# 491 counted tiles instead of 363, and the first 32 gathers taken from x itself

## The chip, the cores and the metric

The program runs on one NeuronCore of a Trainium2 chip. TensorE multiplies matrices, VectorE and ScalarE do elementwise work, GpSimd (POOL) issues the gathers, and SyncE and ScalarE issue the plain DMAs; all run side by side and wait for each other by semaphores. The metric is the device time of one execution in microseconds, the median of several runs.

## The reference

Two graph layers on 12,500 nodes with 32 features and 200,000 edges, sorted by destination. Cut to what matters here:

```
h = relu(layernorm(x))
# layer 0: a normalised sum over neighbours
h0  = h * rsqrt(max(out_degree, 1))
agg = segment_sum(h0[src], dst)
x   = x + agg * rsqrt(max(in_degree, 1)) @ W + b
# layer 1: an MLP over every edge
h   = relu(layernorm(x))
msg = concat(h[dst], h[src] - h[dst])
m   = relu(relu(relu(msg @ W1 + b1) @ W2 + b2) @ W3 + b3) @ W4 + b4
x   = x + segment_sum(m, dst) / max(count(dst), 1)
```

`edge_attr_4` isn't used.

## The kernel before

Edges are cut into 1563 tiles of 128 (`NTR`) and 391 chunks of four tiles (`NCH`, `TPC`). The edges are sorted by destination, so the destinations of chunk g lie in a window of 128 nodes that begins near 32 g (`STEP`, `W`); a flag checks this, and a general path behind `tc.If` stands for other data. The order of the instructions on each engine is the one written out (`manual_schedule`); each engine works in order.

**The start** (lines 137 to 445). x is loaded in four pieces, normalised on VectorE with square roots on ScalarE, and written to the table `tab_h` in DRAM, 33 columns with a one in the last. Then the out-degree of every node is counted: for each tile VectorE makes two one-hot matrices of the source number (its high and low part, lines 331 and 332) and TensorE multiplies them into `deg_ps`. Beside this GpSimd gathers the rows of the first 64 chunks (`EARLY`) from `tab_h` into `rows_early`, whose degree factor isn't known yet. When the degrees are there, a second table `tab_hn` is written: the rows times their factor, each as the sum of three bf16 terms, and a one.

**Layer 0's loop** (lines 754 to 772) runs over m from 64 to 302 and takes the edges in three ways at once:

- *Gathered chunks.* Chunks 64 to 299 (`DIR` is 300) are gathered from `tab_hn`, four gathers of 128 rows for each turn of the loop, into one of eight buffers `rows`. Two turns later `sum_rows` multiplies each tile by its one-hot of the destination and adds four chunks into one PSUM bank `ps_late`; `add_rows` then adds the bank to the sums in SBUF (`Sums.add`, line 528: columns that are new are copied by ScalarE, the others added by VectorE).
- *Early chunks.* Every third turn (`LATER`) a `scale_rows` is begun for one of the first 64 chunks. It has steps of one turn each: a load of the source's high parts (`srow`), a one-hot of them, 12 look-up matmuls into the PSUM bank `look`, then four masked reductions that give each edge its factor, the product, and its split into three bf16 terms by turns of ScalarE and VectorE; then the row sums into a bank `ps_early`, and after every fourth chunk the addition.
- *Counted tiles.* The remaining 363 tiles (`ND`, from chunk 300 on) aren't gathered. `count_edges` makes for each tile a matrix of how often each source node meets each of the tile's 13 destinations: one-hots on VectorE (`oh`, `lo`), and for each of three parts ("thirds") a count matmul of 128 x 429 or 128 x 416 into `count_ps` and its eviction to SBUF on ScalarE (lines 738 to 743). `multiply` then multiplies the counts of eight tiles by the whole table, 98 matmuls, five or six behind each third of the next tiles, and puts the result in place with two small matmuls in `st2`.

`stages` and `steps` spread the thirds evenly over the loop's turns. Node updates (`update_nodes`) follow as sums become complete, one step a turn; they write the tables `tab_i` and `tab_j` of layer 1. [...]the loop uses `ps_late`, `ps_early`, `look`, `st2`, two of `count_ps`, one of the node updates, and `kept`.

**Layer 1's loop** gathers all 1563 tiles from `tab_j` and runs the MLP, two chunks a turn. It begins when the last node update has been written.

Of the kernel before, what the change touches and what calls it, by code (L numbers as in the profile page):

```python
# [8 lines left out]
F32 = mybir.dt.float32  # L9
BF16 = mybir.dt.bfloat16  # L10
# [6 lines left out]
P = 128  # L17
# [41 lines left out]
QE = EARLY // (GRP * J)  # L59

DIR = 300
ND = NTR - DIR * TPC
# [18 lines left out]
def gnn_kernel(  # L83
# [73 lines left out]
    for at in pieces:  # L157
        nc.sync.dma_start(xp[:, at, :], parts(xa)[:, at, :])
    nc.scalar.dma_start(src_i, src_t)
    nc.scalar.dma_start(dst_i, dst_t)  # L160
# [44 lines left out]
    nc.gpsimd.memset(w1s[D:, HID:], 0.0)  # L205

# [36 lines left out]
    src_j = stay.tile([P, NT], I32, name="src_j")  # L245

    def gather(tile_ap, table, col):
        nc.gpsimd.indirect_dma_start(  # L248
            out=tile_ap, out_offset=None, in_=table,
            in_offset=bass.IndirectOffsetOnAxis(ap=col, axis=0))  # L250

# [27 lines left out]
    with tc.tile_pool(name="deg", bufs=3) as hp, tc.tile_pool(  # L279
# [31 lines left out]
        deg_ps = pp.tile([P, PART], F32, name="deg_ps")  # L311
        gathered, batches = 0, list(range(0, NTR, HG * HT))

# [9 lines left out]
        for b in batches:  # L323
            to = min(EARLY, -(-EARLY * (b // (HG * HT) + AHEAD_HG) // len(batches)))
            if to > gathered:
                c = slice(gathered * TPC, to * TPC)
                nc.vector.tensor_scalar(src_j[:, c], src_i[:, c], OFF, None, op0=OP.add)
                for g in range(gathered, to):
                    gather_chunk(rows_early[:, g], tab_h[:, :], g)
                gathered = to  # L330
            hi = one_hots("hi", 0, PART, b)
            lo = one_hots("lo", 1, P, b)
            for t in range(b, min(NTR, b + HG * HT)):
                g, i = divmod(t - b, HT)
                nc.tensor.matmul(deg_ps, lo[:, g, :, i], hi[:, g, :, i], start=(t == 0), stop=(t == NTR - 1))
        nc.vector.tensor_scalar(src_j[:, EARLY * TPC :], src_i[:, EARLY * TPC :], OFF, None, op0=OP.add)
        deg = hp.tile([P, PART], F32, name="deg", bufs=1)
# [243 lines left out]
    with tc.tile_pool(name="e0", bufs=8) as sp, tc.tile_pool(name="nu", bufs=1) as np_, tc.tile_pool(  # L581
# [28 lines left out]

        def hot_ahead(g, name="hot", bufs=AHEAD + 4):
            hots[g] = one_hots(sp, rel_h[:, g * TPC : (g + 1) * TPC], W, name, bufs)

        def sum_rows(g):
            k, i = divmod(g, GRP)
            if i == 0:
                group_ps[k] = pp.tile([D3, SPAN], F32, name="ps_late" if g >= EARLY else "ps_early")
            ps, rows, hot = group_ps[k], rows_of.pop(g), hots.pop(g)
            for t in range(TPC):
                nc.tensor.matmul(  # L620
                    ps[:, STEP * i : STEP * i + W], rows[:, t, :], hot[:, t // 2, :, t % 2], start=(i == 0 and t == 0),
                    stop=(i == GRP - 1 and t == TPC - 1), skip_group_check=True)
# [8 lines left out]
        def scale_rows(g):  # L631
# [5 lines left out]
            turned = sp.tile([PART, CHUNK], BF16, name="sturned", bufs=2)  # L637
            nc.vector.tensor_scalar(turned, row, part_s[:PART], None, op0=OP.is_equal)
            yield
            ps = pp.tile([P, TPC, P], F32, name="look")  # L640
            for t in range(TPC):
# [5 lines left out]
            for t in range(TPC):  # L647
# [5 lines left out]
            scaled = ps[:, 0, :].rearrange("p (t c) -> p t c", t=TPC)  # L653
            nc.vector.tensor_tensor(
                scaled, rows_early[:, g, :, :D], w[:, :, None].to_broadcast([P, TPC, D]), op=OP.mult)
            rows = rows_of[g] = sp.tile([P, TPC, D3], BF16, name="rows_scaled", bufs=2)
            nc.scalar.activation(rows[:, :, 3 * D :], rows_early[:, g, :, D:], AF.Copy)
            for k in range(3):
                part = rows[:, :, k * D : (k + 1) * D]
                nc.scalar.activation(part, scaled, AF.Copy)  # L660
                if k < 2:
                    nc.vector.tensor_sub(scaled, scaled, part)
            hot_ahead(g, "hot_e", 2)
            yield
            sum_rows(g)
            yield
            add_rows(g)

# [53 lines left out]
        def count_edges():  # L722
# [4 lines left out]
            for i in range(ND):  # L727
                g, t = divmod(i, TD)
                if t == 0:
                    for _ in before:  # L730
                        yield
                    if g > 0:
                        before = multiply(g - 1)
                    counts[g] = dp.tile([P, TD, PART, WD], BF16, name="count", bufs=2)
                if i % 2 == 0 and i + 2 < ND:
                    onehots_of(i + 2)
                oh, lo = onehots[i // 2], los[i // TPC]
                for k, (a, b) in enumerate(THIRDS):
                    n = (b - a) * WD
                    ps = pp.tile([P, KW], F32, name="count_ps", bufs=2)  # L740
                    nc.tensor.matmul(ps[:, :n], lo[:, i % TPC // 2, :, i % 2], oh[:, k, :n, i % 2], start=True, stop=True)  # L741
                    nc.scalar.activation(  # L742
                        counts[g][:, t, a:b, :], ps[:, :n].rearrange("p (h d) -> p h d", d=WD), AF.Copy)
                    next(before, None)
                    yield
# [337 lines left out]
```

## Time and profile before

| what | value |
|---|---|
| median of 3 runs | 4330.28 us (4326.65 to 4355.74) |
| the profiled execution | 3552.55 us |
| its span, first to last instruction | 3550.7 us |
| mean granted TensorE clock | 0.812 |
| first gather from `tab_h` (256 in all) | 48.56 us |
| first gather of `rows` (944) | 375.85 us |
| first gather of `gj` (1563) | 1572.77 us |
| last gather of `gj` starts at | 3522.8 us |
| count matmuls (1089), first and last start | 329.6 and 1467.0 us |

A line of the page's groups gives the source line, the engine, the operation with what it writes and reads, how often, the busy time and the mean of one, and the idle time of that engine just before with what ended most of it. A busy share says nothing of what an engine waits for; the views of waits and of single instructions do. POOL's gathers are DMAs[...].

### The profile page before, as it was taken

To read this page: it belongs to the slowest core of one execution; us is meant where nothing else is said; L and a number is where in the kernel's file an instruction comes from. 1 tells how busy PE (TensorE), PEld (TensorE's weight loads), DVE (VectorE), ACT (ScalarE), POOL (GpSimd) and SP (SyncE) were. 2 spreads that over 40 slices of the span, in tenths; PEclk is the share of its full clock that TensorE was granted. 3 is DMA by queue.
4 is the path that set the end of the run, shared out by engine and by line. 5 is a ranking of instruction groups with operands and counts; after the bars stand their busy time and mean duration, and the time that the engine had idled before them with its cause. 6 is when DMAs were issued, how large, how long until landed. Compare 5 with 4: busy or idle time off the path is not lost. (4 is left out here: it accounts for less than half of the span.)

```text
span 3550.7 us, 50481 instructions
## 1 busy us (share of the span) xinstructions
PE 2630.5 (74%) x18596; PEld 1780.9 (50%) x18596; DVE 1669.8 (47%) x4150; ACT 1103.2 (31%) x2552; POOL 2616.8 (74%) x2782
## 2 busy tenths in 40 slices
PE   3871567777777777637888788877788877887787
PEld 2650355555555555514555555544455545554455
DVE  8995456667666665313333333333333333333333
ACT  0002355656656655301212222222212222222212
POOL 3777777777777777767777777777777777777775
PEclk9999998888888888657767877778867788778878
DMA  4113111111211111212222222222222222222221
GB/s 88 15 15 76 24 28 31 32 35 33 38 30 34 33 34 27 45 34 59 61 61 62 61 61 61 61 59 60 61 61 62 61 61 61 61 58 61 61 61 32
DMA packets 238327, 173.61 MB, mean 49 GB/s; under 512 B 157666, under 2 KB 186562, under 8 KB 238074
## 3 DMA queue, kind: packets, MB, share of 16 engines
q0 software_dynamic: 88416, 79.16, 12.4%
q1 hardware_dynamic: 131306, 85.26, 8.8%
q10 hardware_dynamic: 18352, 5.89, 0.9%
q8 instruction: 150, 2.46, 0.3%
q14 instruction: 103, 0.84, 0.1%
HBM read 157.18 MB, written 12.92 MB: 48 GB/s over the span
## 5 line engine op out<-in xcount | busy, mean ns | idle before, releaser
L248 POOL DMA_INDIRECT gj<-tab_j,src_j x1563 | 1474.9, 944 | 493.8 <-issue 414.8
L248 POOL DMA_INDIRECT rows<-tab_hn,src_j x944 | 891.8, 945 | 287.7 <-issue 200.5
L742 ACT ACTIVATE count<-count_ps 128x429 bf16<-128x429 f32 x1089 | 545.0, 525 | 368.7 <-PE count_ps L741 347.1
L845 PE MATMUL p<-ident,gj 128*128 128x128 f32 x784 | 243.6, 351 | 400.6 <-DMA gj<-tab_j,src_j 398.8
L878 DVE TENSOR_TENSOR h<-p,b3n 128x512 f32<-128x512 f32 x196 | 135.3, 690 | 811.5 <-PE p L875 811.5
L875 PE MATMUL p<-w3s,h 128*128 128x64 f32 x3128 | 483.0, 319 | 0.0
L875 PEld LDWEIGHTS p<-w3s,h 128*128 128x128 f32 x3128 | 453.9, 231 | 50.2 <-issue 41.2
L866 ACT ACTIVATE h<-p,b2s 128x512 f32<-128x512 f32 x391 | 247.3, 683 | 739.5 <-PE p L863 739.5
L741 PE MATMUL count_ps<-oh,lo 128*128 128x429 bf16 x1089 | 433.1, 409 | 47.2 <-ACT count L742 33.1
L845 PEld LDWEIGHTS p<-ident,gj 128*128 128x128 f32 x784 | 118.0, 161 | 662.4 <-issue 641.4
L696 PEld LDWEIGHTS <-table 128*128 128x128 bf16 x4508 | 352.3, 109 | 132.2 <-issue 74.8
L696 PE MATMUL st<-count,table 128*128 128x104 bf16 (+1 forms) x4508 | 414.9, 233 | 0.1
L620 PE MATMUL ps_late<-hot,rows 128*97 128x128 bf16 x944 | 166.3, 255 | 306.7 <-DMA rows<-tab_hn,src_j 243.7
L893 PEld LDWEIGHTS ps<-hot,h 128*64 128x64 f32 x3126 | 277.5, 193 | 170.1 <-issue 157.0
L248 POOL DMA_INDIRECT rows_early<-tab_h,src_j x256 | 246.7, 964 | 124.4 <-issue 53.3
L853 ACT ACTIVATE h<-p 128x512 f32<-128x512 f32 x196 | 117.0, 597 | 689.4 <-PE p L849 689.4
L849 PE MATMUL p<-turned,ai 128*64 128x512 f32 x782 | 322.3, 915 | 0.0
L893 PE MATMUL ps<-hot,h 128*64 128x128 f32 x3126 | 306.4, 361 | 0.5 <-DVE h L878 0.5
L685 DVE TENSOR_TENSOR oh<-keys,kept 128x858 bf16<-128x858 f16 x546 | 291.7, 590 | 7.0 <-PE count_ps L741 6.9
L620 PEld LDWEIGHTS <-rows 128*97 128x97 bf16 x944 | 103.5, 138 | 361.5 <-DMA rows<-tab_hn,src_j 293.3
L863 PE MATMUL p<-h,w2s 64*128 64x512 f32 x782 | 263.9, 755 | 0.0
L829 DVE TENSOR_TENSOR turned<-row,kept 128x512 f32<-128x512 f16 x391 | 249.8, 680 | 25.1 <-PE p L849 20.3
(186 smaller groups left out, 2426.2 us busy)
## 6 DMA issues: line engine op xcount, KB each, us to landing
row<-rel_row SPq DMA_DIRECT2D x195, 256.0 KB
gj<-tab_j,src_j POOLq DMA_INDIRECT x1563
rows<-tab_hn,src_j POOLq DMA_INDIRECT x944
ai<-tab_i SPq DMA_DIRECT2D x195, 64.0 KB
srow<-hi_row SPq DMA_DIRECT2D x64, 98.0 KB
rows_early<-tab_h,src_j POOLq DMA_INDIRECT x256
tab_j<-nu_aij SPq DMA_DIRECT2D x24, 128.0 KB
tab_i<-nu_aij SPq DMA_DIRECT2D x24, 128.0 KB
```

The source lines that it names most:

```text
L248: nc.gpsimd.indirect_dma_start(out=tile_ap, out_offset=None, in_=table, in_offset=bass.IndirectOffsetOnAxis(ap=col, axis=0))
L620: nc.tensor.matmul(ps[:, STEP * i : STEP * i + W], rows[:, t, :], hot[:, t // 2, :, t % 2], start=(i == 0 and t == 0), stop=(i == GRP - 1 ...
L685: nc.vector.tensor_tensor(oh[:, k, :n], keys[:, k, None, i : i + 2].to_broadcast([P, n, 2]), count_h[:, :n], op=OP.is_equal)
L696: nc.tensor.matmul(ps[:, : tiles * WD], table[:, h, :], c[:, :tiles, h, :], start=(h == 0), stop=(h == PART - 1))
L741: nc.tensor.matmul(ps[:, :n], lo[:, i % TPC // 2, :, i % 2], oh[:, k, :n, i % 2], start=True, stop=True)
L742: nc.scalar.activation(counts[g][:, t, a:b, :], ps[:, :n].rearrange("p (h d) -> p h d", d=WD), AF.Copy)
L829: nc.vector.tensor_tensor(turned, v["row"][:, k], part_f.to_broadcast([P, CHUNK]), op=OP.is_equal)
L845: nc.tensor.matmul(p1[:, t, :], v["gj"][:, t].rearrange("p k c -> p (k c)"), ident, is_transpose=True, start=(t == 0), stop=False, skip_gr ...
L849: nc.tensor.matmul(p1[k * HID : (k + 1) * HID].rearrange("p t e -> p (t e)"), v["ai"][:, k], v["turned"][k], start=False, stop=True, skip_ ...
L863: nc.tensor.matmul(p2s[k], w2s[s, :], v["h1"][s, :], start=True, stop=True)
L875: nc.tensor.matmul(p3[:, k * TPC + t, :], v["h2"][k][:, t * P : (t + 1) * P], w3s, start=True, stop=True)
L893: nc.tensor.matmul(ps[k * HID : (k + 1) * HID, o : o + W], v["h3"][:, k * TPC + t, :], v["hot"][k][:, t, :], start=(i == 0 and t == 0), st ...
```

## The change

- `DIR` goes from 300 to 268: chunks 64 to 267 are gathered (816 gathers instead of 944), and 491 tiles instead of 363 are counted. The loop over m has 32 turns fewer, and `stages` and `steps` follow.
- `count_ps` has three banks instead of two.
- The bank comes from `ps_early`, which is gone: each early chunk's row sums go into columns of its own `look` bank and are added chunk by chunk.
- The first 8 chunks (`RAW`) are gathered from x itself (`xa`), straight after the memsets on GpSimd and before the layer norm, with the unshifted indices `src_i`; the load of `src_i` is cut so that their 32 columns come first. The ones in the last column are written by a memset. `scale_rows` normalises these rows edge by edge: mean and variance of each gathered row, and the factor times 1 / sd. The product takes the positive part in the same instruction, for all early chunks.
- The spread of the other early gathers over the degree count begins at chunk 8.

```diff
+RAW = 8
-DIR = 300
+DIR = 268
...
-    nc.scalar.dma_start(src_i, src_t)
+    for c in (slice(0, RAW * TPC), slice(RAW * TPC, NT)):
+        nc.scalar.dma_start(src_i[:, c], src_t[:, c])
...
+    nc.gpsimd.memset(rows_early[:, :RAW, :, D:], 1.0)
+    for c in range(RAW * TPC):
+        gather(rows_early[:, c // TPC, c % TPC, :D], xa, src_i[:, c : c + 1])
...
-        gathered, batches = 0, list(range(0, NTR, HG * HT))
+        gathered, batches = RAW, list(range(0, NTR, HG * HT))
...
-            to = min(EARLY, -(-EARLY * (b // (HG * HT) + AHEAD_HG) // len(batches)))
+            to = min(EARLY, RAW + -(-(EARLY - RAW) * (b // (HG * HT) + AHEAD_HG) // len(batches)))
...
-        nc.vector.tensor_scalar(src_j[:, EARLY * TPC :], src_i[:, EARLY * TPC :], OFF, None, op0=OP.add)
+        for c in (slice(0, RAW * TPC), slice(EARLY * TPC, NT)):
+            nc.vector.tensor_scalar(src_j[:, c], src_i[:, c], OFF, None, op0=OP.add)
...
-                group_ps[k] = pp.tile([D3, SPAN], F32, name="ps_late" if g >= EARLY else "ps_early")
+                group_ps[k] = pp.tile([D3, SPAN], F32, name="ps_late")
...
+            h = rows_early[:, g, :, :D]
+            if g < RAW:
+                m = sp.tile([P, TPC], F32, name="raw_m", bufs=2)
+                nc.vector.tensor_reduce(m, h, AX.X, OP.add)
+                nc.vector.tensor_scalar(m, m, 1.0 / D, None, op0=OP.mult)
+                nc.vector.tensor_sub(h, h, m[:, :, None].to_broadcast([P, TPC, D]))
+                square = sp.tile([P, TPC, D], F32, name="raw_sq", bufs=2)
+                nc.scalar.activation(square, h, AF.Square)
             yield
+            if g < RAW:
+                nc.vector.tensor_reduce(m, square, AX.X, OP.add)
+                nc.vector.tensor_scalar(m, m, 1.0 / D, EPS, op0=OP.mult, op1=OP.add)
+                sd = sp.tile([P, TPC], F32, name="raw_sd", bufs=2)
+                nc.scalar.activation(sd, m, AF.Sqrt)
...
-            nc.vector.tensor_tensor(
-                scaled, rows_early[:, g, :, :D], w[:, :, None].to_broadcast([P, TPC, D]), op=OP.mult)
-            rows = rows_of[g] = sp.tile([P, TPC, D3], BF16, name="rows_scaled", bufs=2)
+            if g < RAW:
+                nc.vector.reciprocal(m, sd)
+                nc.vector.tensor_tensor(w, w, m, op=OP.mult)
+
+            nc.vector.scalar_tensor_tensor(
+                scaled, h, 0.0, w[:, :, None].to_broadcast([P, TPC, D]), op0=OP.max, op1=OP.mult)
+            rows = sp.tile([P, TPC, D3], BF16, name="rows_scaled", bufs=2)
...
-            hot_ahead(g, "hot_e", 2)
+            hot = one_hots(sp, rel_h[:, g * TPC : (g + 1) * TPC], W, "hot_e", 2)
             yield
-            sum_rows(g)
+            total = ps[:D3, 1]
+            for t in range(TPC):
+                nc.tensor.matmul(
+                    total, rows[:, t, :], hot[:, t // 2, :, t % 2], start=(t == 0), stop=(t == TPC - 1))
             yield
-            add_rows(g)
+            sums.add(slice(0, D3), STEP * g, total)
+            added([g])
...
-                    ps = pp.tile([P, KW], F32, name="count_ps", bufs=2)
+                    ps = pp.tile([P, KW], F32, name="count_ps", bufs=3)
```

## The prediction

> **What bounds the kernel now.** I read the page's busy rows and slices first, then the costliest groups, then the waits inside the stage that the change touches, then single instructions there.
>
> ```profile
> PE 2630.5 (74%) x18596; PEld 1780.9 (50%) x18596; DVE 1669.8 (47%) x4150; ACT 1103.2 (31%) x2552; POOL 2616.8 (74%) x2782
> ...
> POOL 3777777777777777767777777777777777777775
> ...
> L248 POOL DMA_INDIRECT gj<-tab_j,src_j x1563 | 1474.9, 944 | 493.8 <-issue 414.8
> L248 POOL DMA_INDIRECT rows<-tab_hn,src_j x944 | 891.8, 945 | 287.7 <-issue 200.5
> ```
>
> POOL shows the same digit from the first gather to the end. A 7 is not slack: each gather is 944 ns of work and 0.30 us of "issue", so one starts every 1.248 us, and a slice of such gathers is a 7. The view of POOL in order of time shows that, and a hole at the start:
>
> ```profile
> 48.56 1.10 POOL L248 DMA_INDIRECT rows_early<-tab_h,src_j  x1 [44.20 <-DMA b3n<-in_b]
> 49.96 0.95 POOL L248 DMA_INDIRECT rows_early<-tab_h,src_j  x1 [0.30 <-issue]
> 51.21 0.94 POOL L248 DMA_INDIRECT rows_early<-tab_h,src_j  x1 [0.30 <-issue]
> ```
>
> 2763 gathers of 1.248 us are 3448 of the span's 3550.7 us; the rest is mostly this hole, 18 us between the two layers and 28 us behind the last gather. So the gathers set the time, and only in layer 0's loop (375.9 us, the first gather of `rows`, to 1572.8, the first of `gj`) does the change take any away. What the other engines have left there is told by the waits between 400 and 1460 us (engine, line, what was waited for: us in total, times, longest):
>
> ```profile
> ACT count L742 <- PE count_ps L741: 297.0, 349, 4.0
> PEld L620 <- DMA rows<-tab_hn,src_j: 190.2, 207, 3.1
> ...
> PE ps_late L620 <- DMA rows<-tab_hn,src_j: 155.1, 177, 2.9
> ...
> DVE look L662 <- ACT rows_scaled L660: 112.7, 126, 4.4
> ...
> PE ps_late L620 <- ACT acc_t L542: 55.9, 31, 5.1
> ...
> PE count_ps L741 <- ACT count L742: 26.3, 46, 3.9
> ```
>
> TensorE waits for gathered rows for 155 to 190 of these 1060 us (its two rows see partly the same gap). That is all the slack there is: take gathers away and give counts, and it is used up. The same stretch by engine (busy us and count of PE, PEld, DVE, ACT, POOL; clock; DMA):
>
> ```profile
> 400.00:1460.00 1060.00, 795.60 (x7717) 591.73 (x7714) 660.57 (x2099) 634.23 (x1618) 801.58 (x849) 0.85 0.18 32
> ```
>
> **Two rules of the Trainium skill.** "TensorE: Matmul & The Clock Gate", section on HAM oscillation, says that a gap of more than about 3.4 us puts TensorE back to half clock, and that it then needs about as long to recover. The trace agrees:
>
> ```profile
> 902.63 0.58 PE L620 MATMUL ps_late<-hot,rows 128*97 128x128 bf16 x4 [3.72 <-ACT acc_t L542]
> ...
> 908.57 2.46 ACT L742 ACTIVATE count<-count_ps 128x416 bf16<-128x416 f32 x5 [0.17 <-PE count_ps L741]
> ```
>
> After the 3.72 us gap a third of a counted tile (one count matmul and five or six table matmuls) takes 0.79 us; from 908.6 on it takes 0.49, which is also ScalarE's pace (five evictions in 2.46 us). I go by these two numbers. "SBUF — State Buffer", section "Who interferes with whom", says that VectorE operations in a two-port mode, or with two SBUF inputs, block GpSimd. The 32 new gathers lie beside the layer norm, which is full of such operations. The trace of before doesn't show a cost: between 100 and 200 us VectorE is busy for 100.00 us and POOL starts 81 gathers, the same as elsewhere. I go by the trace.
>
> **The change, part by part.** Sums are made against the profiled execution: 3552.55 us, the span and 1.85 us around it. The median of the runs, 4330.28, is 778 us longer, and no view shows where. I carry the difference in microseconds over unchanged, and price the other reading as a rival.
>
> (1) 32 raw gathers. They need `xa` and 32 columns of `src_i`, whose load is now first on ACT's queue, and are issued behind the memsets that end at 4.4 us. 32 x 1.248 = 39.9 us fit into the hole of 44.2, so the other 224 early gathers start at 48.6 as before and end 39.9 us sooner. Next comes `tab_hn`: its last write is issued at 290.5 us, so the row gathers can start at 336 instead of 375.9. Gain at POOL 39.9 us (bounds: 0, if the gathers were blocked, to 44.2). One more memset (nearest, `hx` 0.32 us) and one more DMA issue on ACT's queue (nearest, SP's of `srow`, 0.31 to 0.34 us) lie in the hole; the added `src_j` operation (0.2 us) is before any gather that reads it.
>
> (2) 128 gathers fewer: 128 x 1.248 = 159.7 us of POOL. With (1), gathers alone would put the first `gj` at 1572.8 - 199.6 = 1373.
>
> (3) 128 counted tiles more: 384 thirds (384 count matmuls, 384 evictions, 1568 table matmuls), 16 more groups with their two transposes, and 192 VectorE one-hots of 0.59 us and 32 of 0.41. On VectorE 126 us, on ScalarE 384 x 0.49 = 188, on TensorE the same 188. Against it stand 128 row-sum matmuls fewer, in 32 iterations fewer of the loop.
>
> (4) TensorE's chain. 1060 less 155 to 190 us of gather waits is 870 to 905 us for 1048 thirds and 212 loop iterations. The thirds at 0.49 us are 514; the remaining 356 to 391 us (row sums, look-ups, node updates, stalls, cold clock) are 1.68 to 1.84 per iteration. After: 1473 x 0.49 = 722, and 204 x 1.68 to 1.84 = 343 to 375, in all 1065 to 1097, middle 1081. Counting begins at 329.6 us, and nothing ahead of it changes but some 1 us for longer keys; so it ends near 1411. The loop's last sums, the last group and the last node updates follow; of before only the last part shows unpaced (last row gather at 1554.0 to `gj` at 1572.8, 18.8 us), so I take 35 (bounds 19 and 60). First `gj` at 1446: 127 us sooner. Chain (1411 + 35) and gathers (1373) don't add; the later one counts.
>
> (5) The third count bank. It can win at most the 26.3 us that TensorE waits for an eviction, and some of the clock; below nothing it can't go, since it only removes waits.
>
> (6) Early sums by chunk. 64 additions instead of 16: VectorE + 48 x 0.25 = 12 us, ScalarE + 64 x 0.19 - 16 x 0.27 = 8 us, both with idle time (VectorE 400 of 1060 us, ScalarE 426). But the sum now lies in `look`'s only buffer, so the next chunk's 12 look-up matmuls wait for the addition issued just ahead of them. Behind them stand four row sums and all counts. The nearest row is the wait for `acc_t` (55.9 / 31 = 1.8 us, longest 5.1). ScalarE's copy stands behind at most three evictions, 1.5 us. Bounds 0 to 64 x 5.1 = 326 us; I take 64 x 0.4 = 26, which (5) pays.
>
> (7) Normalising eight chunks: on VectorE 8 x (0.29 + 0.17 + 0.31 + 0.29 + 0.18 + 0.17 + 0.16), the node update's rows of the same shapes, 12.6 us; on ScalarE 8 x (0.31 + 0.21) = 4.2. Hidden by the same idle time; if it is gone, 17 us.
>
> Sum: -127 us, 3425 for a profiled execution, **4203** for the median. ScalarE then has 92 us (634.2 less 542.5 of evictions) + 722 + 12 = 826 us of work in 1081, VectorE 331 (660.6 less 329.5 of one-hots for 349 tiles) + 329.5 x 491 / 349 + 25 = 820. All three are near their limit, and waits that were harmless can show.
>
> **Rivals.** *The gathers still set the pace.* If the unexplained 778 us lie in the gathers (0.28 each, 1.53 us in an unprofiled run), 816 row gathers take 1248 us, the chain's 1081 hide behind them, and the change gives 128 x 1.53 + 44 = 240: 4090. For it: nothing else is repeated evenly enough. Against: the profile shows 1.248 everywhere.
>
> *The coupling eats the gain.* ScalarE and VectorE wait for each other in each scaled chunk (112.7 and 46.0 us of waits), three engines work in order at 75 to 80%, and the chain comes to some 1180 us: 4300, no change that can be told.
>
> *Slower, by the look-up bank.* At (6), each scaled chunk costs what the wait for `acc_t` cost at its worst in the quoted lines, 3.7 us, enough to drop the clock: 64 x 3.7 = 237 instead of 26, 4330 - 127 + 211 = 4414. It decides from 2.4 us a chunk (26 + 127 = 153 over 64); over 1% slower from 3.1. For it: ScalarE is in order, and copies stand behind evictions. Against: with three banks that queue is short.
>
> *Slower, by the clock.* If the 778 us are a TensorE at half clock in unprofiled runs, it is the bound, and 384 x 0.79 less 128 x 0.15 gives +284: 4614. The profile's 0.85 speaks against it.
>
> **How the numbers follow.** Likeliest, the chain at 4155 to 4270: 0.43. Gathers pace, 4080 to 4130: 0.27. Coupling, within 43 us (1%, about what measuring this kernel can tell from no change): 0.15. Slower: look-up bank 0.10, clock 0.05. So faster 0.70, same 0.15, slower 0.15. The range 4080 to 4320 leaves out the slower cases and the ends of the others.
>
> **What would show it.** First gather near 5 us; first row gather near 336; first `gj` near 1446, then unchanged to the end; in the loop fewer than 81 gathers per 100 us, POOL waiting for TensorE's row sums rather than only for "issue"; TensorE's wait for rows almost gone; clock above 0.85. Wrong would be: 81 gathers per 100 us all the way and `gj` near 1373; look-up matmuls waiting over 2 us for the `acc_e` copy; a gap between median and profile that changes by more than 50 us.

## The result: 51 us slower, and two kinds of chip

The changed kernel takes **4379.9 us** (median of 9, 4369.8 to 4386.8) beside 4328.9 for the kernel before (median of 9, 4316.3 to 4355.7). The ratio is **1.0109** [1.0087, 1.0130]: slower by 1%, where 3% faster had been forecast.

One thing has to be known to read any number below: the kernel before takes about 4330 us on some chips and about 3551 us on others, steadily, and the profiled execution of the prediction (3552.55 us) was of the second kind while the times it forecast from (4330.28) were of the first. Of the five chips that ran the experiments, one was of the 3551 kind and four of the 4330 kind. Each was used in one session, so the runs can't tell a lasting property of a chip from a state that it was in; "kind of chip" stands for either. Every kernel is compared with the kernel before on the same chip; "beside 4330" and "beside 3551" say which kind that was.

### The profile page after: what moved, and what is told of

The parts are those of the page before. It is cut to its first block, busy times and chain, and to the rows that moved or that the text cites. A ratio compares the mean times of both kernels' runs of the same rounds, so it can differ in the third digit from the quotient of the medians.

```text
span 4370.6 us, 54919 instructions
## 1 busy us (share of the span) xinstructions
PE 2953.7 (68%) x20468; PEld 1939.2 (44%) x20468; DVE 1792.5 (41%) x4473; ACT 1279.9 (29%) x3034; POOL 2501.2 (57%) x2655
## 4 chain that ended last, share of the span: by engine, by line
PE 35%; another core or an unknown queue 11%; issue 10%; DVE 4%; POOL 3%; ACT 2%; DMA 1%; ACTq 0%; DVEq 0%; POOLq 0%
PE p L905 9%; PE p L893 6%; PE p L879 5%; PE ps L923 5%; PE p L875 3%; POOL gj L211 3%; PE count_ps L771 2%; PE st L726 2%; ACT count L772 1%; DVE hot L575 1%; DVE turned L859 1%; DVE h L908 1%; PE kept L836 1%; PE ps_late L628 0%
## 5 line engine op out<-in xcount | busy, mean ns | idle before, releaser
L211 POOL DMA_INDIRECT rows<-tab_hn,src_j x816 | 771.8, 946 | 793.2 <-PE ps_late L628 281.5
L772 ACT ACTIVATE count<-count_ps 128x429 bf16<-128x429 f32 x1473 | 716.9, 527 | 508.4 <-PE count_ps L771 289.1
L771 PE MATMUL count_ps<-oh,lo 128*128 128x429 bf16 x1473 | 585.5, 421 | 180.7 <-ACT count L772 69.1
L726 PEld LDWEIGHTS <-table 128*128 128x128 bf16 x6076 | 480.2, 110 | 328.7 <-issue 254.4
L726 PE MATMUL st<-count,table 128*128 128x104 bf16 (+1 forms) x6076 | 565.4, 234 | 14.3 <-ACT acc_d L550 6.3
L893 PE MATMUL p<-h,w2s 64*128 64x512 f32 x782 | 384.4, 840 | 70.6 <-issue 69.0
L715 DVE TENSOR_TENSOR oh<-keys,kept 128x858 bf16<-128x858 f16 x738 | 393.7, 589 | 80.5 <-PE count_ps L771 39.0
L342 PE MATMUL deg_ps<-hi,lo 128*128 128x98 bf16 x1563 | 175.8, 271 | 195.1 <-DVE lo L325 147.3
L575 DVE TENSOR_TENSOR hot<-rel_h,kept 128x512 f32<-128x512 f16 x391 | 249.2, 678 | 0.0
L342 PEld LDWEIGHTS <-lo 128*128 128x128 bf16 x1563 | 131.0, 126 | 240.0 <-DVE lo L325 177.1
```

The lines of the kernel that those rows point to most:

```text
L211: nc.gpsimd.indirect_dma_start(out=tile_ap, out_offset=None, in_=table, in_offset=bass.IndirectOffsetOnAxis(ap=col, axis=0))
L715: nc.vector.tensor_tensor(oh[:, k, :n], keys[:, k, None, i : i + 2].to_broadcast([P, n, 2]), count_h[:, :n], op=OP.is_equal)
L726: nc.tensor.matmul(ps[:, : tiles * WD], table[:, h, :], c[:, :tiles, h, :], start=(h == 0), stop=(h == PART - 1))
L772: nc.scalar.activation(counts[g][:, t, a:b, :], ps[:, :n].rearrange("p (h d) -> p h d", d=WD), AF.Copy)
L893: nc.tensor.matmul(p2s[k], w2s[s, :], v["h1"][s, :], start=True, stop=True)
```

## The profile after

The page of the changed kernel, taken beside 4330: busy rows, POOL's slices, and the two groups of gathers.

```profile
PE 2953.7 (68%) x20468; PEld 1939.2 (44%) x20468; DVE 1792.5 (41%) x4473; ACT 1279.9 (29%) x3034; POOL 2501.2 (57%) x2655
...
POOL 6554355444554444554666666666666666666663
...
L211 POOL DMA_INDIRECT gj<-tab_j,src_j x1563 | 1477.9, 946 | 882.3 <-issue 437.8
L211 POOL DMA_INDIRECT rows<-tab_hn,src_j x816 | 771.8, 946 | 793.2 <-PE ps_late L628 281.5
```

POOL is no longer a row of 7s. A gather still takes 0.946 us, but half of POOL's time in layer 0 is waiting, and most of that is not "issue". In layer 1, where nothing was changed, it waits too. The waits from 400 to 2030 us (engine, line, what was waited for: us in total, times, longest):

```profile
POOL rows L211 <- PE ps_late L628: 281.5, 70, 6.5
...
DVE look L687 <- ACT rows_scaled L685: 193.3, 105, 7.0
POOL rows L211 <- issue: 191.5, 624, 0.6
POOL rows L211 <- PE count_ps L771: 184.9, 76, 6.6
...
PE look L664 <- ACT acc_e L550: 89.0, 45, 3.8
...
POOL rows L211 <- PE c_ps L451: 62.0, 1, 62.0
```

The gathers wait for TensorE, 281.5 us for the row sums that free their buffers and 184.9 for counts. TensorE's wait for gathered rows, 155 us in the profile of the prediction, is not among the longer waits. One wait of 62 us for `c_ps`, a small product behind the degree stage, holds the first row gather until 480.8 us. The look-up matmuls wait 89 us for the addition of the early sums: that line is new, and it is the one that the prediction had named as a sign of being wrong (over 2 us each was its mark; 89.0 / 45 is 2.0).

How different the two kinds of chip are shows best in the degree stage, in code that the change leaves alone. Below are the stretches 60 to 260 and 500 to 1900 us of the changed kernel (busy us and count of PE, PEld, DVE, ACT, POOL; clock; DMA share; GB/s), and after them 60 to 260 us of two kernels whose degree stage is that of the kernel before: `half_gj`, an experiment below, beside 4330, and the kernel before itself, profiled again on the chip of the 3551 kind.

```profile
60.00:260.00 200.00, 93.72 (x835) 69.72 (x832) 117.19 (x238) 0.00 (x0) 115.53 (x123) 1.00 0.13 14
500.00:1900.00 1400.00, 987.20 (x9451) 727.00 (x9450) 766.37 (x2365) 799.04 (x2064) 708.75 (x750) 0.81 0.14 22
```

```profile
60.00:260.00 200.00, 84.82 (x755) 63.31 (x756) 106.44 (x221) 0.00 (x0) 121.72 (x129) 1.00 0.11 12
```

```profile
60.00:260.00 200.00, 164.03 (x1463) 122.40 (x1462) 200.00 (x426) 0.00 (x0) 150.91 (x160) 1.00 0.13 15
```

835 and 755 matmuls against 1463 in the same 200 us, all at a granted clock of 1.00; VectorE is busy 117 and 106 us rather than 200. No instruction takes longer on VectorE, ScalarE or POOL (a gather 946 ns and 944, the 128x512 eviction on ScalarE 685 and 684); the time lies between the instructions.

## Experiments

Times are medians in us; the ratio is to the kernel before on the same chip. "First `gj`" is where layer 1's gathers begin.

| kernel | beside | time | ratio | first row gather | first `gj` |
|---|---|---|---|---|---|
| before_now | 3551 | 3554.9 | one run | 374.6 | 1571.4 |
| raw_only | 3551 | 3516.7 | 0.9906 [0.9889, 0.9922] | 338.7 | 1536.4 |
| counted_only | 3551 | 3525.7 | 0.9930 [0.9913, 0.9947] | 377.9 | 1546.2 |
| banks_only | 3551 | 3551.3 | 1.0003 [0.9994, 1.0012] | 375.3 | 1572.2 |
| changed_now | 4330 | 4391.7 | 1.0144 [1.0111, 1.0177] | 481.5 | 2035.1 |
| changed_b | 4330 | 4386.5 | 1.0131 [1.0091, 1.0170] | 482.2 | 2037.3 |
| changed_c | 4330 | 4377.5 | 1.0114 [1.0090, 1.0139] | 480.6 | 2029.8 |
| raw_only_b | 4330 | 4302.9 | 0.9944 [0.9930, 0.9958] | 479.9 | 1949.9 |
| raw_counted | 4330 | 4348.1 | 1.0051 [1.0032, 1.0069] | 477.0 | 1993.9 |
| two_banks | 4330 | 4402.1 | 1.0174 [1.0152, 1.0196] | 479.3 | 2049.1 |
| banks_only_b | 4330 | 4332.8 | 1.0002 [0.9985, 1.0020] | 506.1 | 1977.1 |
| after_284 | 4330 | 4317.9 | 0.9977 [0.9961, 0.9992] | 481.6 | 1966.3 |
| after_332 | 4330 | 4438.0 | 1.0265 [1.0240, 1.0289] | 474.6 | 2083.6 |
| half_table | 4330 | 4220.7 | 0.9732 [0.9696, 0.9769] | 483.3 | 1875.2 |
| half_rows | 4330 | 4089.0 | 0.9443 [0.9422, 0.9464] | 479.2 | 1732.0 |
| third_bf16 | 4330 | 4276.0 | 0.9879 [0.9837, 0.9922] | 504.7 | 1984.4 |
| half_gj | 4330 | 3362.6 | 0.7779 [0.7750, 0.7808] | 502.1 | 1971.5 |
| raw_third | 4330 | 4249.2 | 0.9818 [0.9787, 0.9850] | 479.8 | 1953.6 |

**The kernel before again: where are the 778 us?** No edit.

> The kernel before, unedited, profiled once more. Theory A (the profiled execution of 3552 us was not like the timed ones, and every stage of a timed one is longer by stalls of the consuming engines): a span near 4330 us, the first row gather at some 420 to 480 us rather than 375.9, the first gj at some 1950 to 2000 us, and POOL waiting over 200 us for the row sums in layer 0's loop, as in the profile of the changed kernel. Rival B (the two kernels really differ as the two profiles show, and 778 us lie outside the profiled span): a span near 3550 us again, the first gj near 1573, POOL waiting for 'issue' only.

Its span was 3553.1 us on a chip where its timed runs take 3551. The span is the one that rival B expected, but the timed runs there take 3551 us too, so no 778 us lie outside it, and both A and B fall for this chip. The changed kernel's profiled span, 4370.6 us, likewise agrees with its own timed runs. The gap was not between profiled and timed executions; it was between chips.

third_bf16 and half_gj, below, are the kernel before up to the end of layer 0, so their traces tell where it stands beside 4330: first row gather at 503 us rather than 375 (+128), first `gj` at 1971 to 1984 rather than 1571 (another +273 to +283). Layer 1's gathers then span 2314 to 2332 us in every trace beside 4330 that leaves it alone, 2320 in the middle, rather than 1950 (+370). Together that is the gap.

**The parts, beside 3551.**

```diff
-DIR = 300
+DIR = 268
```

> Only DIR = 268, so 128 tiles are counted that were gathered; early sums in groups, two count banks, no raw gathers. Theory A (in a timed execution TensorE, ScalarE and VectorE set the pace of layer 0, and a counted tile costs them more than its gather saved): slower than before, by 50 to 120 us (128 x 0.4 to 0.9). Rival C (the slowdown is that of the early sums in the look-up bank): this part alone is faster by 50 us or more. The recorded forecast by its own steps: some 100 us faster.

25 us faster, so neither theory A, nor rival C, nor the forecast's 100 us. The waits from 400 to 1460 us show what the removed gathers left:

```profile
POOL rows L248 <- issue: 171.8, 562, 0.6
...
POOL rows L248 <- PE count_ps L741: 113.6, 104, 5.9
PE count_ps L741 <- ACT count L742: 106.9, 100, 4.7
...
POOL rows L248 <- PE ps_late L620: 30.2, 17, 4.3
```

The gathers now wait for TensorE, and TensorE for ScalarE's evictions: 107 us rather than the 26.3 of before. Counting lasts from 333.6 to 1471.8 us and the first `gj` comes 74 us after that.

The raw gathers alone (the new gathers, their normalising, the split index load; DIR 300, two banks, early sums in groups):

> Only the 32 raw gathers with their normalising; DIR stays 300, early sums in groups, two count banks. Theory A: the end of the early gathers is not what the row gathers wait for (that is VectorE and TensorE in the degree stage), so within 20 us of the kernel before. The recorded forecast by its own steps: POOL ends 39.9 us sooner, so 20 to 44 us faster.

34 us faster; theory A falls. Layer 0's row gathers of this kernel (count, min/median/max ns, first and last start):

```profile
L211 POOL DMA_INDIRECT rows<-tab_hn,src_j x944: 940/944/1063, 338.7 to 1516.6; - x189
```

They start at 338.7 us rather than 374.6. Here the forecast's step held.

The third bank and the early sums by chunk, at DIR 300:

```diff
-                    ps = pp.tile([P, KW], F32, name="count_ps", bufs=2)
+                    ps = pp.tile([P, KW], F32, name="count_ps", bufs=3)
...
-            sum_rows(g)
+            total = ps[:D3, 1]
+            for t in range(TPC):
+                nc.tensor.matmul(
+                    total, rows[:, t, :], hot[:, t // 2, :, t % 2], start=(t == 0), stop=(t == TPC - 1))
             yield
-            add_rows(g)
+            sums.add(slice(0, D3), STEP * g, total)
+            added([g])
```

> Only the third count bank and the early sums by chunk in the look-up bank; DIR stays 300, no raw gathers. Theory A: the two are near even, -30 to +30 us. Rival C (each scaled chunk stalls TensorE for the addition): slower by 64 x 2 to 64 x 4 = 128 to 256 us, with look-up matmuls waiting over 2 us for the acc_e copy. The recorded forecast: 0, since 26 us are won and 26 lost.

No difference. The look-up matmuls' wait for the addition is there (27.3 us, 57 times, longest 1.0), beside 178.5 us of TensorE's waits for gathered rows, behind which it is probably hidden. The third bank's own gain is in the same zero, so the recorded forecast's reading, as much won as lost, is not excluded.

**The whole, and the parts again, beside 4330.**

> The changed kernel, unedited, beside a kernel before of the same session. In the session of the first experiments the kernel before takes 3551 us, as its profiled execution did, not 4329. Theory A2 (two conditions of the chip: at 3551 the gathers are near the bound and the change gains; at 4329 every stage of TensorE, VectorE and ScalarE is drawn out, gathers wait for them, and the change loses 51 us): if the kernel before takes 3551, the changed one takes 3491 or less (raw gathers -34, counted tiles -25, added), and 3425 if the recorded forecast's sum held. If the kernel before takes 4329, the changed one takes 4380. Rival D (the changed kernel itself falls into the drawn-out form, whatever the session): 4370 beside 3551.

> The changed kernel, unedited, once more, for a session of the other kind: so far the kernel before took 3551 us in the first session and 4331 in the second, on another chip, while the parts were measured in the first and the whole in the second. Theory F (a chip on which TensorE is held back takes 4331; there the end of layer 0 is TensorE's, on the other the gathers'): where the kernel before takes 3551, the changed one takes 3491 or less (the sum of the parts, -59), and where it takes 4331, 4380 to 4392 again. Rival D (the changed kernel itself falls into the drawn-out form): 4370 or more in both.

> The changed kernel, unedited. It has been timed on chips where the kernel before takes 4330, never where it takes 3551. Theory F: 3491 or less beside 3551; 4380 to 4392 beside 4330.

All three came to stand beside 4330 and repeat the result: +49 to +60 us. So rival D is not excluded by them: the whole change was never timed beside 3551, where its parts add up to -58 (-34, -25, +1).

The raw gathers alone:

> Only the 32 raw gathers, DIR 300, two count banks, early sums in groups; for a session of the other kind. Theory F: beside 3551 it was 3517 (-34). Beside 4331 the row gathers wait for the degree stage's TensorE (62 us in the changed kernel's trace), so -10 to +10. The recorded forecast by its own steps: -20 to -44 in both.

26 us faster, within the forecast's -20 to -44, and theory F's -10 to +10 fell. The first row gather comes 22 to 26 us sooner (479.9 against 502.1 to 506.1 in the kernels with the early gathers of before) although it waits 61 us for `c_ps`.

The third bank and the early sums by chunk at DIR 300:

> Only the third count bank and the early sums by chunk, DIR 300; for a session of the other kind. Beside 3551 it was 3551 (0). Theory G (on the chip where TensorE is held back, the early sums in the look-up bank lengthen a chain that nothing hides): 20 to 60 us slower than before, since with 491 tiles the changed kernel was 44 slower than the same kernel with groups and two banks. Rival (the 44 us are only of the many counted tiles): -15 to +15.

Nothing in sum, as the rival said. So what costs in the whole must need the 491 tiles. The changed kernel with early sums in groups and two banks, and with early sums by chunk and two banks:

> The changed kernel with two count banks and early sums in groups: the raw gathers and the 128 further counted tiles alone. Theory A2: the bank is worth more with 491 tiles than with 363, since counts waited 102 us for evictions in the kernel with counted tiles only (26 us before): 10 to 60 us slower than the changed kernel. Rival C (early sums by chunk cost TensorE stalls, hidden while gathers set the pace, visible with 491 tiles): 20 to 100 us faster than the changed kernel.

> The changed kernel with two count banks rather than three; early sums by chunk in the look-up bank stay. Beside 4330 the same kernel with groups and two banks took 4348, the changed one 4386 to 4392, so 40 us lie in one of the two. Theory G (the early sums in the look-up bank): 4380 to 4400, no better than the changed kernel. Rival J (the third bank lets counts run ahead of the row sums that free the gathers' buffers): 4340 to 4355. Beside 3551: theory F says 5 to 40 us slower than the changed kernel.

Going from kernel to kernel by the ratios (1% is 43 us; the whole at the mean of its three, 1.0130):

- 32 raw gathers: 0.9944, -24 us
- 128 counted tiles more: 0.9944 to 1.0051, **+46 us**
- early sums by chunk, at 491 tiles and two banks: 1.0051 to 1.0174, **+53 us**
- the third bank: 1.0174 to 1.0130, -19 us

Sum +56, by construction the mean of the three repeats (the first result was +51). The kernels stood on different chips of the kind; the changed kernel's own three ratios scatter by 13 us. Two differences can be taken on one chip: two_banks is 25 us above changed_c, and changed_now 44 above raw_counted (+53 - 19 by the ratios). Theory G holds where tiles are many: two_banks came out above the changed kernel, not at 4340 to 4355, so the bank helps and the early sums cost. Two lines of the waits of two_banks, 400 to 2040 us:

```profile
PE count_ps L771 <- ACT count L772: 110.6, 137, 4.5
...
PE look L664 <- ACT acc_e L550: 57.8, 45, 3.1
```

With groups the second line doesn't exist. The first is 117.8 us there, so the early sums do not show in the counts' own wait; they put the look-up's wait ahead of everything behind it on TensorE.

**Which way do counted tiles pay?** The changed kernel with 64 or 256 tiles moved back to gathers:

```diff
-DIR = 268
+DIR = 284
```

> The changed kernel with DIR = 284: 64 tiles fewer are counted and 64 more gathered, 80 us of POOL at 1.248 us each. Theory A2, session of 3551: the engines, not the gathers, end layer 0 at DIR = 268, so within 20 us of the changed kernel, faster by up to 20; session of 4329: faster than the changed kernel by some 20 to 30 us (half of what 128 tiles cost). Rival E (gathers still set the pace at DIR = 268): slower than the changed kernel by up to 80 us.

```diff
-DIR = 268
+DIR = 332
```

> The changed kernel with DIR = 332: 256 tiles fewer are counted (235 in all) and 256 more gathered, 320 us of POOL. Theory A2, session of 3551: gathers alone set layer 0, from 336 us on 1072 row gathers of 1.248 us, so the first gj near 1680 and some 3660 us in all, 170 slower than the changed kernel. Session of 4329: POOL is waiting there anyway, so faster than the changed kernel by 30 to 100 us. Rival E: slower by 320 us in both.

At 284 it is 74 us faster than the changed kernel on the same chip, over twice what was expected, and 10 us faster than before. At 332 it is slower than both, where 30 to 100 us less had been expected: fewer counts and more gathers there do not mean less time. In the stretch 500 to 1900 us of after_332 (same columns as before) TensorE is busy a quarter less than in the changed kernel, and its granted clock is 0.63 rather than 0.81:

```profile
500.00:1900.00 1400.00, 749.31 (x5771) 572.14 (x5771) 574.30 (x1986) 441.71 (x1249) 889.06 (x941) 0.63 0.16 26
```

So a tile's price is not one number. Of the three values tried with the changed kernel 284 is the best; 300 was run only with parts of the change. Why 332 is so bad was not taken apart.

**TensorE or gathers?** The changed kernel without every second table matmul, so that its counted sums are incomplete:

```diff
-                    nc.tensor.matmul(
-                        ps[:, : tiles * WD], table[:, h, :], c[:, :tiles, h, :], start=(h == 0), stop=(h == PART - 1))
+                    if h % 2 == 0:
+                        nc.tensor.matmul(
+                            ps[:, : tiles * WD], table[:, h, :], c[:, :tiles, h, :], start=(h == 0), stop=(h == PART - 2))
```

> The changed kernel without every second table matmul (L726: 49 of the 98 of each counted group, so 3038 of 6076, some 263 us of TensorE's busy time at 0.087 us each; the counted sums are then incomplete). All gathers, evictions and one-hots stay. Theory F, beside 4330 (layer 0 ends with TensorE): first gj 150 to 300 us sooner, 4090 to 4240. Rival K (ScalarE, VectorE or semaphores end it): within 50 us of the changed kernel. Beside 3551: 50 to 150 us sooner than the changed kernel, down to where the gathers of layer 0 end (first gj 1373).

The changed kernel with half of layer 0's row gathers; the rows of two tiles stand in for four, so its sums are other numbers:

```diff
-                gather_chunk(rows_of[m], tab_hn[:, :], m)
+                for t in range(TPC // 2):
+                    c = m * TPC + t
+                    gather(rows_of[m][:, t, :], tab_hn[:, :], src_j[:, c : c + 1])
...
-                    ps[:, STEP * i : STEP * i + W], rows[:, t, :], hot[:, t // 2, :, t % 2], start=(i == 0 and t == 0),
+                    ps[:, STEP * i : STEP * i + W], rows[:, t % 2, :], hot[:, t // 2, :, t % 2], start=(i == 0 and t == 0),
```

> The changed kernel with two gathers for each chunk of layer 0's loop rather than four; the row sums read each gathered tile twice, so TensorE, ScalarE and VectorE have the same work and POOL 408 x 1.248 = 509 us less. Theory F, beside 4330: the gathers are hidden behind TensorE, so within 40 us of the changed kernel (4340 to 4400). Rival (the gathers still set the pace of layer 0): 4000 to 4250. Beside 3551: between; if TensorE ends layer 0 there too, within 30 us.

half_table gives 157 us for 3038 matmuls, as theory F said. half_rows gives **289 us** for 408 gathers, and theory F fell. The time is in the rival's range, yet that gathers set the pace does not fit the trace: in the changed kernel no wait of TensorE for gathered rows is among the longer ones, and in half_rows POOL waits longer for TensorE than it did with all gathers (526 us for counts alone between 500 and 1600 us, 143 before). The stretch 500 to 1600 us, first of changed_c, then of half_rows:

```profile
500.00:1600.00 1100.00, 768.71 (x7363) 567.29 (x7363) 597.01 (x1841) 619.54 (x1605) 555.06 (x589) 0.82 0.14 22
```

```profile
500.00:1600.00 1100.00, 852.67 (x9234) 639.61 (x9234) 745.41 (x2312) 759.67 (x2021) 340.78 (x360) 0.91 0.11 19
```

With 229 gathers fewer in the stretch, TensorE gets through 9234 matmuls rather than 7363. The gathers slow TensorE without its waiting for their data. This does not hang on the releasers, of which the traces beside 4330 miss many (half_gj has 20,392 semaphore updates on record, before_now 63,134): all the idle time in front of the row sums is 87.8 us in the changed kernel, and 297.2 in before_now, where the gathers do set the pace.

**The same in layer 1, where nothing else of the change lies.** The kernel before with half of layer 1's gathers (each gathered tile is used twice):

```diff
-                gather_chunk(gj[:, :, k, :], tab_j[:, :], g)
+                for t in range(min(TPC // 2, NTR - g * TPC)):
+                    c = g * TPC + t
+                    gather(gj[:, t, k, :], tab_j[:, :], src_j[:, c : c + 1])
...
-                    p1[:, t, :], v["gj"][:, t].rearrange("p k c -> p (k c)"), ident, is_transpose=True,
+                    p1[:, t, :], v["gj"][:, t % 2].rearrange("p k c -> p (k c)"), ident, is_transpose=True,
```

> The kernel before with two gathers for each chunk of layer 1 rather than four (782 rather than 1563); TensorE's transposes read each gathered tile twice, so all other work is the same. Theory L (beside 4330 the gathers' traffic itself holds TensorE back: in the degree stage TensorE starts 7.3 matmuls per us where little is gathered and 2.9 where much is, beside 3551 it is 7.2 and 7.3): layer 1, 2317 us there and TensorE's by its waits, comes near the 8 to 9.5 us of TensorE work in each of 196 steps, 1570 to 1860 us, so 3570 to 3900 in all. Rival M (TensorE is held back there by itself, whatever is gathered): it waits for gathers for only some 30 us of layer 1, so within 60 us of the kernel before. Beside 3551 both say 3170 to 3450, since there layer 1 has the gathers' pace.

970 us faster. Theory L holds, and the gain is beyond its range: rival M's 60 us is far off. Layers 0 of the two kernels agree (first `gj` at 1971.5 and, with all gathers, 1977 to 1984), so this is not a better chip. In layer 1, first changed_c (2100 to 4300 us), then half_gj (2100 to 3300):

```profile
2100.00:4300.00 2200.00, 1630.60 (x8272) 967.73 (x8272) 639.62 (x1263) 396.27 (x777) 1404.91 (x1490) 0.70 0.23 51
```

```profile
2100.00:3300.00 1200.00, 1097.26 (x7830) 724.28 (x7832) 600.84 (x1202) 358.28 (x742) 656.29 (x697) 0.91 0.30 69
```

6.5 matmuls per us rather than 3.8. A step of layer 1 (196 of them) takes 6.9 us of the span of the gathers rather than 11.8. The clock rises too, from 0.70 to 0.91; whether that is a cause or follows from fewer standstills isn't separated. Here again TensorE was not waiting for the data: its idle time before the matmuls that read gathered rows, first in before_now, then in the changed kernel, is the smaller on the slow kind.

```profile
L845 PE MATMUL p<-ident,gj 128*128 128x128 f32 x784 | 244.3, 350 | 407.0 <-DMA gj<-tab_j,src_j 405.1
```

```profile
L875 PE MATMUL p<-ident,gj 128*128 128x128 f32 x784 | 210.1, 365 | 177.7 <-issue 136.8 <-DMA gj<-tab_j,src_j 39.5
```

The degree stage has no such test, but the same association, with a delay. Counted by half microseconds from 60 to 400 us of half_gj, TensorE starts 2.1 matmuls per us where six or more gathers began in the 8 us before, and 6.2 where at most four did. In before_now six or more stand before nearly every stretch, and it starts 7.3.

**Less work for TensorE in layer 1.** The kernel before with the third product in bf16:

```diff
+    nc.scalar.activation(w3b, w3s, AF.Copy)
...
-                h2 = ep.tile([P, CHUNK], F32, name=f"h2{k}")
+                h2 = ep.tile([P, CHUNK], BF16, name=f"h2{k}")
...
-                        p3[:, k * TPC + t, :], v["h2"][k][:, t * P : (t + 1) * P], w3s, start=True, stop=True)
+                        p3[:, k * TPC + t, :], v["h2"][k][:, t * P : (t + 1) * P], w3b, start=True, stop=True)
```

> The kernel before with the messages' third product in bf16 (h2 written as bf16, a bf16 copy of w3): the 16 matmuls of a step in layer 1 take some 0.5 us rather than 2.0, gathers and all else stay, and the rounding differs. Theory F: where the kernel before takes 3551, layer 1 has the pace of its gathers (1563 x 1.248 = 1950 us), and nothing changes, -10 to +10; where it takes 4331, layer 1 is TensorE's, and 196 steps with 1.5 us less give -100 to -300. Rival H (there the gathers or the semaphores of layer 1 are slow, not TensorE's work): within 30 us in both.

53 us, less than theory F's 100 and more than rival H's 30: 0.27 us a step of the 1.5 that the expectation counted. What may take its place shows in order of time. From layer 1 of this kernel, all engines (start us, us, engine, line, operation, and in brackets the idle time before and its releaser):

```profile
3053.62 0.64 PE L851 MATMUL p<-turned,ai 128*64 128x512 f32 x1
3054.49 0.66 PE L851 MATMUL p<-turned,ai 128*64 128x512 f32 x2 [0.23 <-issue]
...
3055.91 0.59 PE L851 MATMUL p<-turned,ai 128*64 128x512 f32 x1 [0.75 <-issue]
...
3063.42 0.94 POOL L248 DMA_INDIRECT gj<-tab_j,src_j  x1 [0.30 <-issue]
3064.67 0.94 POOL L248 DMA_INDIRECT gj<-tab_j,src_j  x1 [0.30 <-issue]
3068.64 0.69 DVE L880 TENSOR_TENSOR h<-p,b3n 128x512 f32<-128x512 f32 x1 [17.53 <-remote]
3068.74 1.26 ACT L868 ACTIVATE h<-p,b2s 128x512 bf16<-128x512 f32 x2 [15.05 <-remote]
3069.10 0.94 POOL L248 DMA_INDIRECT gj<-tab_j,src_j  x1 [3.49 <-remote]
...
3069.39 0.91 PE L895 MATMUL ps<-hot,h 128*64 128x128 f32 x6 [12.89 <-DVE h L880]
```

Between matmuls of one group TensorE pauses for 0.23 and 0.75 us, for "issue" alone. Then TensorE, VectorE and ScalarE stand still for over 12 us while POOL goes on gathering until its buffers are full. 3 us after its last gather VectorE, ScalarE and POOL are released within half a microsecond. By the program all three wait for TensorE, whose matmuls for VectorE had ended at 3052.0 by the trace. Standstills come about every 23 us here. One ended alike, with releases at 3022.65, 3022.75 and 3023.11; the one between them ended in two steps, VectorE at 3041.36 while POOL was still gathering, ScalarE and POOL at 3045.63 and 3045.94. The trace can't say whether the matmuls or their signals were late: ends of matmuls are modelled, and "remote" means that no record names the releaser. That the work which bf16 removes from TensorE mostly lengthens the standstills fits this, but was not measured over the layer.

**A version that beats both.** Raw gathers alone with the bf16 product:

> The version that the runs point to: the 32 raw gathers alone (DIR 300, two count banks, early sums in groups) and the third product in bf16. Beside 4330 the parts gave -26 and -53, so 4240 to 4270 if they add; beside 3551 -34 and about 0, so 3510 to 3525. Theory L: the bf16 product is worth less than its 1.5 us in each step, since the gathers' traffic stays; theory F: they add in full.

84 us faster than before (0.9818), as the two parts add up to (-26 and -53). The raw gathers alone need no change of precision and are faster than the kernel before on both kinds of chip (3516.7 and 4302.9), and than the changed one beside 4330.

## Why the prediction was wrong

The step that failed is the carrying over: "The median of the runs, 4330.28, is 778 us longer, and no view shows where. I carry the difference in microseconds over unchanged." The difference was no constant ahead of or behind the work. It was a chip on which every stage with gathers in it runs longer, 128 us before the loop, 273 to 283 in layer 0's loop and 370 in layer 1. The slack that was to pay for the counted tiles, 155 to 190 us of TensorE's waits for rows, was slack of the other kind of chip: beside 4330 no such wait is among the longer ones, in the changed kernel or in half_gj, whose layer 0 is that of the kernel before. The forecast took -127 for raw gathers and tiles together, +26 for the early sums and -26 for the bank; beside 4330 these came to +22 (-24 and +46), +53 and -19.

Step by step:

1. **Raw gathers, -39.9: right.** -34 beside 3551 and -26 beside 4330. The 32 gathers take 1.45 us each, not 1.248 (6.1 to 52.5 us in raw_only), so the next one starts 3.9 us past the hole; 39.9 less 3.9 is the 35.9 us by which the row gathers start sooner. The prediction had set aside what the Trainium skill's "SBUF — State Buffer", section "Who interferes with whom", says of VectorE operations with two SBUF inputs and a GpSimd instruction that reads SBUF (a gather reads its indices there). The trace of raw_only agrees with it (start us, us, engine, line, operation):

```profile
36.17 1.23 DVE L253 SCALAR_TENSOR_TENSOR hx<-hx,la_v 112x1024 f32<-112x1024 f32 x1
36.33 1.88 POOL L211 DMA_INDIRECT rows_early<-in_xa,src_i  x1 [0.30 <-issue]
...
38.77 1.23 DVE L245 TENSOR_TENSOR hx<-xp,la_m 112x1024 f32<-112x1024 f32 x1
39.76 1.05 POOL L211 DMA_INDIRECT rows_early<-in_xa,src_i  x1 [0.31 <-issue]
```

All twelve gathers that start inside such an operation of the layer norm (lines 245, 246 and 253) end 0.81 or 0.82 us behind it, however early in it they began. That is 4.6 us of the 6.4 beyond 32 x 1.248; most of the rest lies beside the shifts and casts of the source numbers. The stretch from 100 to 200 us, where the prediction had looked for a cost, couldn't show this one: its one-hots have their second input (`lane_g`) in PSUM.

2. **Gathers alone, -159.7: right as a price, not as a gain.** 0.944 + 0.30 us stayed on both kinds of chip, but POOL was no longer what the end of layer 0 waited for.
3. and 4. **TensorE's chain: mis-sized even beside 3551.** In counted_only it begins at 333.6 as forecast (329.6), and ends at 1471.8, not 1411; the tail is 74 us, not 35. That leaves 26 of the forecast 127 us without the raw gathers. Iterations cost (1138 - 722) / 204 = 2.04 us, not 1.68 to 1.84: TensorE waited 107 us for evictions with two banks (without these it would be 1.51), and row gathers ran until 1507.2 because they waited for TensorE. The whole kernel has a third bank, so this bound may be looser for it. Beside 4330 the same tiles cost 46 us.
5. **Third bank, at most 26.3: near.** 19 us at 491 tiles beside 4330.
6. **Early sums by chunk, 26 taken: the mechanism right, the size not.** 53 us with 491 tiles, 0.8 us a chunk rather than 0.4, measured with two banks; there the waits for the `acc_e` copy sum to 57.8 us, 1.3 each time (45), and in the changed kernel to 89.0, 2.0 each time. The rival that ended slower by this had priced it at 237 less 127 of gain. The sign was as that rival said; the price was a quarter, and the gain it was set against didn't exist there.
7. **Normalising, hidden:** no run speaks against it. raw_only contains it, and of the 35.9 us by which its row gathers start sooner 34 are left at the end.

Of the rivals, "the gathers still set the pace" was nearest to naming gathers as the source of the 778 us, for the wrong reason: a gather took no 1.53 us, but 0.94 and 0.30 to the next where nothing held it. "By the clock" saw TensorE as held back, but the granted clock of the stretch 60 to 260 us is 1.00 in all three profiles. The forecast's sign that the gap between median and profile would tell came true: it vanished. Two signs of being right came true as well, POOL waiting for row sums and TensorE's wait for rows gone, but they say nothing for the forecast: in layer 0 of half_gj, the kernel before's, POOL waits 112.4 us for row sums and TensorE for no rows that show.

## What to carry to other kernels

Where a profiled execution and the timed runs differ by 18%, no slack read from that profile may be spent in a forecast of the others; profile the kernel where it is timed first. An exchange between two engines (here gathers for counted tiles) is worth its price only on the chip where the engine relieved is the one that ends last, so a part that only removes work from a wait (the raw gathers) is safer than one that trades. And sharing a buffer between two steps can cost nothing in one setting (0 at DIR 300, together with the third bank) and show in another (53 us at DIR 268); that another wait covers it in the first is likely, not shown.

## What was not expected of the hardware

- Two kinds of chip, or states that last a session: one program takes 3551 or 4330 us, each within 1% on its kind, with equal durations of instructions on VectorE, ScalarE and POOL.
- On the slower kind gathers from DRAM by GpSimd hold TensorE back without its waiting for them: 782 gathers fewer made layer 1's gathers span 1359 us rather than 2320, 408 fewer made the changed kernel 289 us shorter. The Trainium skill's "SBUF — State Buffer", section "Who interferes with whom", says that a DMA never contends with a compute engine and that TensorE waits on no one, but it says so of the ports of SBUF, and no run shows that a port is what holds TensorE back here; so it is neither confirmed nor refuted. Whether it is the traffic, POOL's own work for a gather, late signals between engines, or power was not tried.
- On the kind of 3551 none of it shows: 1463 matmuls in the 200 us of the degree stage beside 160 gathers, 755 beside 129 on the other.
- A gather that starts inside a VectorE operation with two inputs in SBUF is held until near its end (twelve of twelve in raw_only, up to 1.89 us rather than 0.94).
